# A new table of offsets for the planner that orders a graph network's steps

## The chip, the cores and the metric

The kernel runs on one core of one Trainium2 chip. The core has a matrix engine (TensorE, PE in the profile; its weight loads are PEld), a vector engine (VectorE, DVE), a scalar engine (ScalarE, ACT), GpSimd (POOL) and a queue for transfers (SyncE, SP). Each works through its own list of instructions in order and waits at semaphores for the others. The metric is the device time of one execution in microseconds (us).

## The reference, cut to what matters

The input is 128 graphs of 64 nodes with 128 features, and a weighted adjacency matrix for each. Four layers follow each other, each of them a layernorm, a relu, a graph network and a residual:

- layer 0 makes, for every edge, 64 Gaussians of the edge weight, a softplus of a 64 to 128 matrix product, a second product, and sums neighbours' features times this filter;
- layer 1 works in hyperbolic space: each node's feature is mapped by norms, tanh and artanh; for every edge a silu of a product, a score through a sigmoid, and a weighted sum of logarithmic maps; then a small network, more norms, tanh and silu;
- layer 2 is a product with the normed adjacency matrix, layer 3 messages averaged over neighbours.

```python
h = jnp.maximum(_layernorm(x, axis=-1), 0.0)
x = x + _L0_gnn_ref(h, adj, adj, ...)
...
x = x + _L1_gnn_ref(h, adj, ...)
x = x + _L2_gnn_ref(h, adj, ...)
x = x + _L3_gnn_ref(h, adj, ...)
```

The result is x after the fourth layer, in float32.

## The kernel before, in words

Eight graphs make a group (two graphs on the 128 partitions, four such pairs), and 16 groups are computed. Since few nodes are joined, the nodes of a graph are sorted by degree and each node has a number of slots for its neighbours; the slots come in three blocks, of 512, 512 and 264 columns a pair. Per-edge work runs over these slots. (A second, dense program stands behind a flag, for inputs with too many neighbours; it isn't run here.)

Each group passes seven stages, written as Python generators: `load` (two transfers), `order` (sorting, one-hot tables `oh`), `layer0` (filters per edge), `layer1_nodes` (norms and maps of the nodes), `layer1_edges` (scores per edge), `rest1` (the end of layer 1) and `rest2` (layers 2 and 3, and the store). A stage starts further generators for its parts: `squares`, `duo`, `filter_of` and `neighbours` belong to `layer0`; `coefs_of`, `rows` and `scores_of` to `layer1_edges`; `one_minus_z`, `attention`, `norm_of_h` to `layer1_nodes`; `product_with_h` to `rest1`. A generator's name with a 2 behind it in the table means the third, smaller block of slots.

A generator yields `on(engine, buffers, after=events, table=...)` ahead of each of its steps: on which engine the step runs, which buffers it takes, what must have been issued before, and whether it needs ScalarE's table of logarithm and exponential ("log") or of silu and tanh ("silu"). The class `Weave` plans: it keeps a modelled time for each engine (`free`, advanced by the costs in `about`, from line 785), and `step` (line 940) looks up, for all generators, when their next step could begin. It takes the engine of the earliest one, and among the steps of that engine which could begin within 0.05 us of it the one with the lowest key. The instructions are emitted in that order, and the kernel's scheduler is told to keep it on four engines. At run time nothing chooses: the order is fixed, and waits follow from the data.

The key is set in `Stream.go_on` (line 860):

```python
self.want = next(self.gen, None)
self.key = self.rank + next(self.late, 0.0)
```

`rank` is twice the group's number plus the stage's due time (`load` -6, `order` -4, `layer0` and `layer1_nodes` -3, `layer1_edges` 0, `rest1` 2, `rest2` 4). `late` runs over the entry of the table `LATE` (line 808) for this generator, one offset per step, and gives 0.0 once that is used up. So a positive number lets other steps go first, a negative one draws a step forward. The offsets are the same for every group.

ScalarE's table is switched by the last loop of `sparse_stack`: for each group it goes silu (until `soft_ready`), log (until `soft`, the softplus of the layer 1 nodes), silu (until the scores and `rest1` are through) and log (until the filters of layer 0 and the nodes are through). Steps of the other table wait.

Of the kernel before, what the change touches and what calls it, by code (L numbers as in the profile page):

```python
# [784 lines left out]
def about(engine, op, args, kw):  # L785
# [14 lines left out]
    if engine == ACT:  # L800
# [5 lines left out]


LATE = {
    "attention": (0, 3.75),
    "coefs_of": (2.5, 0, -0.25),  # L810
    "coefs_of2": (2.5,),
    "duo": (4, 4.25),
    "duo2": (0, 3.5, -1.5),
    "filter_of": (1.75, 3.5, 0.25, -0.75, 0, -2.25),
    "filter_of2": (-3.75, 3.5, 0, 4.5, -2.5),
    "layer1_edges": (0, 0, 0, -3),
    "layer1_nodes": (-2.25, 0, 0, 0, 0, 4.5, 0, 4.25, 1.75, 0, 0, 0, 0, 0, 3.5, 0.5, 0, 0, 0, 0, 0,
        0, 0, 0, -1.5, 0, 0, 0, 0, -3.25, 0, 0, 0, 0, 0, 0, -0.5, 0, 0, 0, 0, 0, 0, 3, 0, 0, 3),
    "neighbours": (-0.5, -2),
    "neighbours2": (3.5,),  # L820
    "one_minus_z": (-1.5,),
    "order": (0, 0, -2.25, 0, 0, 0, 4.25, 3.25, 0, -2, 0, 1.75, 0, 2.25, 0, 0, 1.75, 0, 6, -2.25),
    "product_with_h": (0, 2.5),
    "rest1": (0, 0, 0, -3.75, 0, 0, 0, 1, 0, -3.25, 0, 0, 0, 0, -0.5, -2, 0, 0, 0, 0, 0, 0, -1.25),
    "rest2": (0, 0, 0, 0, 0, 0, 0, 0, 0, 0, 0, -3.75, 0, 2, 0, 2.75, 0, 0, 0, 0, 3.5, 0, 0, 0, 0, 0,
        0, 0, 1),
    "rows": (1.25, -2.75),
    "rows2": (1.75, -0.25),
    "scores_of": (0.75, 0, -1.75, -0.5),
    "scores_of2": (0, -1.25),  # L830
    "squares": (2,),
    "squares2": (0, 2.25),
}


# [1422 lines left out]
```

## Time and profile before

| | us |
|---|---|
| median of three runs (2148.49 to 2150.37) | 2149.32 |
| profiled execution | 2152.3 |
| its span, first to last instruction | 2150.5 |
| TensorE matmuls busy in the span | 1826.5 (85%), 11223 instructions |
| VectorE busy | 1832.9 (85%), 4829 instructions |
| ScalarE busy | 1671.5 (78%), 3385 instructions |
| GpSimd busy | 369.7 (17%), 362 instructions |
| ScalarE table loads, in the above | 111.6, 87 loads |

The mean granted TensorE clock is 0.941 of full speed. Almost every instruction is issued by the same helper (line 849, in `Timed`), so rows of the profile are told apart by the names of the tiles. In such a row, `out<-in` names the written and the read tiles, then come partitions x elements, the count, busy time, mean duration of one, and the idle time of the engine ahead of them with what ended it. Names that help here: `e` and `ex` are the Gaussians and the wide activations per edge, `ra` the neighbours' features, `two` the filter product of the third block, `va` weights or coefficients per slot, `th` the tanh of the scores, `oh` the one-hot tables, `rt`, `rs`, `bR`, `n`, `Sx` and `nn` tiles of the layer 1 nodes, `w` and `k_` tiles of `rest1`, `big`, `sm` and `sl` PSUM buffers.

### The profile page before, as it was taken

What the parts mean: (1) busy time and instruction counts of PE and PEld (TensorE: products, weight loads), DVE (VectorE), ACT (ScalarE), POOL (GpSimd) and SP (SyncE); (2) the same over time, 40 slices, a digit from 0 to 9 for tenths busy, and PEclk for the clock granted to TensorE, in tenths of its full rate; (3) what the DMA queues carried; (4) which work ended last, traced back from release to release, by engine and by line L of the source; (5) the groups of instructions that cost most, each with busy time, mean ns of one, the idle gap of its engine ahead of it and who ended that gap; (6) DMA issues with size and microseconds to landing.
All of it is one profiled execution on the core that took longest, in us unless ns stands there. A gap on an engine that the chain in (4) does not pass through costs nothing.

```text
span 2150.5 us, 32066 instructions
## 1 busy us (share of the span) xinstructions
PE 1826.5 (85%) x11223; PEld 873.5 (41%) x11223; DVE 1832.9 (85%) x4829; ACT 1671.5 (78%) x3385; POOL 369.7 (17%) x362
## 2 busy tenths in 40 slices
PE   3767989898999989898999989898999989896773
PEld 2223333443444444443444444443444444433342
DVE  4448889899999989899999989899999999887752
ACT  1968787979879797979879797979879797985541
POOL 1000101122120212122120212222130212202121
PEclk9988999999999999999999999999999999998775
DMA  2000000000000000000000000000000000000000
GB/s 52 5 0 6 1 6 1 1 6 8 6 8 6 8 6 8 1 6 8 6 8 6 8 6 8 1 6 8 6 8 1 8 1 6 1 1 6 5 1 12
DMA packets 29532, 13.95 MB, mean 6 GB/s; under 512 B 10544, under 2 KB 29360, under 8 KB 29360
## 3 DMA queue, kind: packets, MB, share of 16 engines
q1 hardware_dynamic: 29360, 11.80, 2.1%
q8 instruction: 90, 1.47, 0.3%
q14 instruction: 82, 0.67, 0.1%
HBM read 7.61 MB, written 4.19 MB: 5 GB/s over the span
## 4 chain that ended last, share of the span: by engine, by line
PE 41%; ACT 31%; DVE 22%; issue 4%; DMA 1%; POOL 0%; SPq 0%; DVEq 0%; ACTq 0%; POOLq 0%
PE big L849 29%; PE sm L849 9%; ACT ex L849 9%; ACT e L849 5%; DVE va L849 4%; ACT ra L849 4%; PE sl L849 4%; ACT n L849 3%; DVE oh L849 3%; DVE ex L849 2%; DVE ah L849 2%; DVE y L849 2%; ACT va L849 2%; ACT L849 2%; ACT th L849 1%
## 5 line engine op out<-in xcount | busy, mean ns | idle before, releaser
L849 PE MATMUL big<-ex,w2T 128*128 128x512 f32 (+1 forms) x768 | 328.5, 553 | 41.3 <-ACT ex L849 35.0
L849 PE MATMUL big<-e,w1T 64*128 64x512 f32 (+1 forms) x768 | 205.3, 635 | 57.2 <-ACT e L849 52.6
L849 ACT ACTIVATE ex<-big,c_L_gnn_att_b 128x1024 f32<-128x1024 f32 (+1 forms) x192 | 183.3, 968 | 78.0 <-PE big L849 77.4
L849 DVE SCALAR_TENSOR_TENSOR ex<-big,c_L_gnn_b,ra 128x1024 f32<-128x1024 f32 x128 | 163.8, 1280 | 67.8 <-PE big L849 55.6
L849 PEld LDWEIGHTS big<-ex,w2T 128*128 128x128 f32 x768 | 131.2, 190 | 215.7 <-ACT ex L849 93.0
L849 ACT ACTIVATE ex<-big,c_L_gnn_b 128x1024 f32<-128x1024 f32 (+1 forms) x192 | 184.6, 978 | 43.9 <-PE big L849 43.6
L849 PE MATMUL big<-va,U 64*128 64x512 f32 (+1 forms) x768 | 184.7, 558 | 31.8 <-DVE va L849 31.6
L849 PE MATMUL big<-va,a 64*128 64x512 f32 (+1 forms) x768 | 185.5, 579 | 10.3 <-DVE two L849 4.3
L849 PE MATMUL sl<-ex,aw2b 128*64 128x512 f32 (+1 forms) x768 | 180.7, 549 | 8.4 <-ACT th L849 4.5
L849 ACT ACTIVATE ra<-big 128x528 f32<-128x528 f32 (+1 forms) x192 | 167.3, 884 | 17.7 <-PE big L849 17.0
L849 ACT ACTIVATE ex<-ex 128x1024 f32<-128x1024 f32 (+1 forms) x192 | 175.6, 924 | 0.9
L849 DVE TENSOR_REDUCE y<-ex 128x128 f32<-128x1024 f32 x128 | 155.1, 1212 | 0.8
L849 POOL TENSOR_TENSOR k_r<-k_r,exp 128x4 f32<-128x4 f32 x32 | 47.5, 1484 | 580.4 <-DVE k_r L849 568.7
L849 ACT ACTIVATE th<-sl,hab 128x512 f32<-128x512 f32 (+1 forms) x192 | 118.1, 615 | 37.0 <-PE sl L849 35.2
L849 PE MATMUL big<-slot_r,Sx 64*128 64x512 bf16 (+1 forms) x1152 | 137.4, 343 | 0.0
L849 PEld LDWEIGHTS big<-e,w1T 64*128 64x128 f32 x768 | 69.4, 205 | 155.6 <-ACT e L849 65.2
L849 ACT ACTIVATE va<-va,sr 128x512 f32<-128x512 f32 (+1 forms) x192 | 122.5, 649 | 9.0 <-DVE va L849 9.0
L849 PE MATMUL big<-oh,pqs 64*64 64x512 bf16 (+1 forms) x1152 | 122.8, 347 | 0.0
L849 ACT ACT_TABLE_LOAD x87 | 111.6, 1283 | 2.2 <-PEq L2246 0.7
L849 DVE COPY_PREDICATED va<-slot_r,big 128x1024 f32<-128x1024 uint16 (+1 forms) x96 | 106.6, 1111 | 5.3 <-PE big L849 5.1
L849 DVE TENSOR_TENSOR va<-oh,adjT 128x1024 f32<-128x1024 bf16 (+6 forms) x160 | 103.6, 697 | 5.7 <-ACT va L849 4.9
L849 DVE TENSOR_TENSOR oh<-pos,slot_k 128x2048 bf16<-128x2048 bf16 (+6 forms) x128 | 107.7, 849 | 0.2
(470 smaller groups left out, 3799.6 us busy)
## 6 DMA issues: line engine op xcount, KB each, us to landing
x<-in_x_dram SPq DMA_DIRECT2D x16, 256.0 KB, 2.9
out_dram<-v SPq DMA_DIRECT2D x16, 256.0 KB, 2.3
adj<-in_adj_dram SPq DMA_DIRECT2D x16, 128.0 KB, 2.3
e<-in_L_gnn_mlp_w_dram SPq DMA_DIRECT2D x3, 64.0 KB, 1.8
wupd<-in_L_gnn_W_upd_dram SPq DMA_DIRECT2D x1, 128.0 KB, 5.8
e<-in_L_gnn_Wd_dram SPq DMA_DIRECT2D x2, 64.0 KB, 2.9
e<-in_L_gnn_W_dram SPq DMA_DIRECT2D x2, 64.0 KB, 1.8
e<-in_L_gnn_att_w_dram SPq DMA_DIRECT2D x2, 64.0 KB, 1.8
```

Of the source, the lines that this page charges most:

```text
L849: return f(*args, **kw)
```

## The change

Only the table `LATE` is replaced. Generators that had no entry get one (`layer0`, `normed_x`, `product_with_bias`, `weights_of2`), some lose theirs (`attention`, `one_minus_z`, `rows`), and nearly all others have other offsets. Costs, due times, buffers, table switching and all steps stay.

```diff
 LATE = {
-    "attention": (0, 3.75),
-    "coefs_of": (2.5, 0, -0.25),
-    "coefs_of2": (2.5,),
-    "duo": (4, 4.25),
-    "duo2": (0, 3.5, -1.5),
-    "filter_of": (1.75, 3.5, 0.25, -0.75, 0, -2.25),
-    "filter_of2": (-3.75, 3.5, 0, 4.5, -2.5),
-    "layer1_edges": (0, 0, 0, -3),
-    "layer1_nodes": (-2.25, 0, 0, 0, 0, 4.5, 0, 4.25, 1.75, 0, 0, 0, 0, 0, 3.5, 0.5, 0, 0, 0, 0, 0,
-        0, 0, 0, -1.5, 0, 0, 0, 0, -3.25, 0, 0, 0, 0, 0, 0, -0.5, 0, 0, 0, 0, 0, 0, 3, 0, 0, 3),
-    "neighbours": (-0.5, -2),
-    "neighbours2": (3.5,),
-    "one_minus_z": (-1.5,),
-    "order": (0, 0, -2.25, 0, 0, 0, 4.25, 3.25, 0, -2, 0, 1.75, 0, 2.25, 0, 0, 1.75, 0, 6, -2.25),
-    "product_with_h": (0, 2.5),
-    "rest1": (0, 0, 0, -3.75, 0, 0, 0, 1, 0, -3.25, 0, 0, 0, 0, -0.5, -2, 0, 0, 0, 0, 0, 0, -1.25),
-    "rest2": (0, 0, 0, 0, 0, 0, 0, 0, 0, 0, 0, -3.75, 0, 2, 0, 2.75, 0, 0, 0, 0, 3.5, 0, 0, 0, 0, 0,
-        0, 0, 1),
-    "rows": (1.25, -2.75),
-    "rows2": (1.75, -0.25),
-    "scores_of": (0.75, 0, -1.75, -0.5),
-    "scores_of2": (0, -1.25),
-    "squares": (2,),
-    "squares2": (0, 2.25),
+    "coefs_of": (2.25, 1.75),
+    "coefs_of2": (2.25,),
+    "duo": (3.25, 3.75, -3.5),
+    "duo2": (1, 2.5),
+    "filter_of": (2, 5, 0, 0, 0.5, -3),
+    "filter_of2": (-2.75, 2.5, -2.25, 2.75),
+    "layer0": (0, 0, 0, 0.25),
+    "layer1_edges": (0, 0, 0, -3.5),
+    "layer1_nodes": (3.75, 0, 0, 2.25, 3, 3, 0, 2.5, 0, 1.5, 0, 0, 0, 0, 0, 0, 0, 3, 0, 0, 0, 0, -3,
+        0, 0, 0, 0, 0, 0, 0, 0, 0, 0, 0, 0, 2.25, -3.75, 2.25, 0, 0, 0, 0, 0, 0, 0, 0, 3.5),
+    "neighbours": (0, -1.5),
+    "neighbours2": (2.25, 2),
+    "normed_x": (0, 0, 0, 0, -3, 2, -3.5),
+    "order": (0, 0, 0, 0, 2.5, 0, 0, -4.25, 0, 4.25, 0, 0, 4, 0, 2, 0, 0, 2.75, 0, 0, 3.25),
+    "product_with_bias": (0, -0.75),
+    "product_with_h": (0, 2.75),
+    "rest1": (0, 1, 0, -3.5, -1.5, 0, 0, -3.5, -0.75, 0, 0, 0, 0, 0, 0, 0, 0, 0, 3.75),
+    "rest2": (8.75, 0, 0, 0, 0, 0.25, 0, 0, 0, 0, 0, -3.25, 0, 0.5, 0, 2.25, 0, 0, -0.5, 0, 4.25, 0,
+        -4, 0, 1.25, 0, -2.5, 0, 5.25),
+    "rows2": (2, -0.25),
+    "scores_of": (-2.5, 1.75, -3.5),
+    "scores_of2": (0.75, 0, 0, 3),
+    "squares": (3, 7.5),
+    "squares2": (2.75, 0, 0, 3.5),
+    "weights_of2": (0, 0.75),
 }
```

## The prediction

> **What bounds the kernel now.** I read the page's forty slices first, then busy time by stretch, then the waits of the busiest engine, then single instructions.
>
> ```profile
> PE   3767989898999989898999989898999989896773
> DVE  4448889899999989899999989899999999887752
> ACT  1968787979879797979879797979879797985541
> PEclk9988999999999999999999999999999999998775
> ```
>
> Three parts: a lead-in of some four slices, a long even middle, and a drain at the end in which nobody is full. In VectorE's records the first instruction of the edges of group 2 starts at 453.8 us and that of group 13 at 1787.2, so one group takes (1787.2 - 453.8) / 11 = 121.2 us. I cut the span there (columns: PE, PEld, DVE, ACT, POOL busy, granted clock, DMA share, GB/s):
>
> ```profile
> 52.00:139.00 87.00, 60.18 (x246) 22.42 (x247) 41.01 (x59) 79.40 (x86) 0.00 (x0) 0.92 0.01 3
> 139.00:222.00 83.00, 61.01 (x291) 29.03 (x291) 62.41 (x162) 60.58 (x124) 6.54 (x7) 0.81 0.01 4
> 454.00:1787.00 1333.00, 1210.40 (x7700) 575.82 (x7699) 1246.65 (x3284) 1123.21 (x2311) 259.45 (x231) 0.98 0.02 6
> 1908.00:2015.00 107.00, 81.66 (x506) 44.27 (x505) 81.45 (x241) 61.42 (x156) 16.74 (x17) 0.81 0.01 3
> 2015.00:2151.00 136.00, 81.56 (x514) 48.31 (x512) 63.14 (x221) 46.21 (x127) 25.25 (x26) 0.66 0.03 7
> ```
>
> From 52 to 139 us ScalarE is the limit (79.4 of 87 us). In the middle it is VectorE: 1246.65 / 11 = 113.3 us of 121.2, so 7.9 us a group are idle. Of these 4.1 us lie in gaps over 0.15 us; the rest are small gaps between instructions. No order can win more in the middle than these 4.1 us a group. After 1908 no engine is full: a chain of dependent steps sets the time. VectorE's waits in the middle:
>
> ```profile
> DVE ex L849 <- PE big L849: 17.7, 27, 1.1
> DVE ex L849 <- ACT ra L849: 8.5, 11, 0.8
> DVE two L849 <- PE big L849: 6.1, 11, 0.6
> DVE dn L849 <- PE sm L849: 4.7, 10, 0.5
> DVE a L849 <- PE sm L849: 3.0, 11, 0.3
> ```
>
> Eleven of each are eleven periods. In one period (1181 to 1302 us) they stand at 1182.07 (0.44 us), 1212.22 (0.27), 1238.65 (0.47), 1261.96 (0.77), 1267.88 (0.21), 1269.61 (0.55) and 1274.03 (1.05), 3.76 us together.
>
> **What the Trainium skill says.** "PSUM — Partial Sum Buffer", section "Engine vs sequencer instructions": the queues of ScalarE, VectorE and GpSimdE are strict FIFO. So an instruction whose input is late holds all behind it, and the order decides which wait is covered. The trace agrees: at 1186.69 ScalarE idles 4.55 us before a Square on `w`, with scores queued behind it. "ScalarE: Activation LUTs", section "What ACT_TABLE_LOAD costs", gives 1283 ns for a table load and 1380 ns more for a drain. The trace has the same load, but no such drain:
>
> ```profile
> L849 ACT ACT_TABLE_LOAD x87 | 111.6, 1283 | 2.2 <-PEq L2246 0.7
> 81.14 1.28 ACT L849 ACT_TABLE_LOAD   x1
> 82.44 0.70 ACT L849 ACTIVATE ex<-big,c_L_gnn_b 128x528 f32<-128x528 f32 x1
> ```
>
> (the two lower lines are ScalarE's timeline.) The next activation follows 0.02 us after the load ends, so I price a load at 1.283 us.
>
> **The change part by part.** It computes nothing else and adds no instruction of work. On every engine the multiset of steps is the same, the DMA queue's order is the same, and VectorE, ScalarE, PE and POOL agree to the letter in their last 218, 110, 329 and 27 steps of the stream. So no engine gets less work except in one place:
>
> 1. *Lead-in.* There Exp and Ln force a load at each alternation between them, until the first switch to silu. The built program before holds 87 loads, as the trace does; after, 83. All four fewer are in this lead-in (26 against 22), because Exp and Ln now more often run in pairs. 4 x 1.283 = 5.1 us of ScalarE. Its share busy there is 79.4 / 87 = 0.91, so I count 0.91 x 5.1 = 4.7 us gained. Bounds: nothing, if the chain of group 0's nodes (139 to 222, where ScalarE has 22 us free) swallows it; 4 x 2.66 = 10.6 us by the skill's dearer price.
>
> 2. *Middle, twelve periods.* I laid VectorE's new order over one period's timeline.
> Covered now: the 0.44 us at 1182.07, since two `coefs_of` products (1.13 us apart) stand ahead of the `filter_of` product instead of one; and the 0.27 us at 1212.22, since the first softplus step of `layer1_nodes` moves behind `rest1`'s artanh, about 8.3 us of VectorE work later. Together -0.71 us.
> The moved softplus keeps its cover: between its halves stand a reduction and four small products (1.13 + 1.05 us), ScalarE needs 1.29. So does the layernorm after it: ahead of its second half stand 0.64 + 1.13 + 0.78 us, POOL's two steps take 1.45. `x` and `ln_mv` thus come later, but what reads them stands where it stood.
> Added: the clamp of `rt` moves from behind `one_minus_z` to right behind one reduction.
>
> ```profile
> 1277.72 0.29 DVE L849 TENSOR_SCALAR rt<-e 128x256 f32<-128x256 f32 x1
> 1277.93 1.21 DVE L849 TENSOR_REDUCE y<-ex 128x128 f32<-128x1024 f32 x1
> 1279.06 0.28 DVE L849 TENSOR_SCALAR bR<-gr 128x256 f32<-128x256 f32 x1
> ```
>
> ScalarE's Ln and two Exp run from 1278.05 to 1279.37; the clamp would start at 1279.06. That is a new wait of 0.31 us and a hop, +0.35 us; behind it are queued `bR`, `e`, and, through `e`, ScalarE's last Ln.
> Also added: the second step of splitting `Sx` moves from 1295.47 to about 1293.5. Its copy on ScalarE, at 1294.66 now, has 0.7 us less work ahead of it after `xp`, a 0.69 us wait that may go, and about 0.4 us less before `xp`: 1292.9 to 1293.5, and 0.54 us long. A wait of 0 to 0.7 us; I take +0.15, the low side, as the copy's own input now comes earlier as well.
> Nought: `ra`, for which VectorE waits at 1261.96, moves behind one more Ln on ScalarE (+0.53 us), but waits of 0.21, 0.55 and 1.05 us follow within 12 us, and for the first two of them that Ln is earlier. If these don't shrink it costs 0.53.
> The one-hot compares and both first `rows` products of the edges change places; they are needed long after, or leave ScalarE's scores nearer together. Neither shows a VectorE wait.
> Sum -0.71 + 0.35 + 0.15 = -0.21 us a period, x 12 = -2.5 us. Bounds: -3.76 x 12 = -45 us, and about +1.6 x 12 = +19 us.
>
> 3. *Drain.* From 1911.1 ScalarE is on the silu table for the last edges but one; it leaves it for the softplus of group 15 at 1919.44 and idles 1.39 us for VectorE there, after idling 2.71 us for `w`. In the new order two scores and a tanh stand ahead of `w`, and the softplus comes after ten scores and tanhs more. I count both waits as gone: -4.1 us. VectorE now reaches group 15's first node step after 20.9 us more of other work, and its norms (`nn`) after 8.1 us more. In the trace `nn` is ready at 1951.9 us and waits for the log table, which comes only after the last tanh (1962.80), so about 10.9 us are free. POOL's `ln_r` there is moved behind `rest1`'s norms (0.27 + 1.04 us), with the same cover. Bounds -8 and +8 us. From group 15's edges to the end (136 us) hardly a step moves.
>
> Sum: -4.7 - 2.5 - 4.1 = -11.3 us. The profiled execution has a span of 2150.5 us and took 2152.3; that becomes 2139.2 and 2141.0. The median shown is 2149.3, 3.0 under the profiled one: 2149.3 - 11.3 = 2138.0 us. What a measurement can tell from no change is about 0.2%, 4.3 us.
>
> **The rivals.**
> *Slower: the `Sx` split.* For it: VectorE is at its limit, so any wait in the middle is paid twelve times. If the copy stays at 1294.66 while the subtraction comes at 1293.5, VectorE stands until 1295.3: 1.8 us instead of 0.15, +1.65 x 12 = 19.8 us, and -11.3 turns to +8.5: 2157.8 us. It ends slower by over 0.2% from a wait of 0.15 + (11.3 + 4.3) / 12 = 1.45 us on. Against it: the copy has less queued ahead.
> *Nothing measurable.* The four loads are hidden by the node chain (0), `ra`'s 0.53 us isn't absorbed (-2.5 + 6.4 = +3.9), the drain gives 4.1: -0.2 us, 2149. For it: idle ScalarE from 139 on.
> *Much faster.* The later waits shrink as well: half of the 3.76 us, 1.9 x 12 = 22.6, and 8.8 from both ends: -31.4, 2118 us. For it: `ex` and `two` wait for PE work whose order changed in many small ways I can't price. Against: the instructions around those waits on VectorE are unmoved.
>
> **How the numbers follow.** The forecast 0.50, slower 0.20, nothing 0.13, much faster 0.17. The forecast's own range is 2125 to 2146, and little of it falls within 0.2%. Faster 0.65, same 0.14, slower 0.21. The range 2114 to 2159 takes in most of the far cases.
>
> **What would show it.** ScalarE with 83 loads of 1.283 us; the edges of group 0 starting some 5 us before 222.1; the period near 121.0; in it no wait of `ex` at the start of the edges nor of `a`, a new one of `rt` for ScalarE of about 0.35 us, and at most 0.7 us for `Sx`; the last tanh before group 15's log table about 4 us earlier, relative to group 14's edges. A period over 121.6 or a wait for `Sx` over 1.45 us makes the forecast wrong; so does one under 120, or a drain that isn't shorter.

## The result, and the profile after

The new table is slower: a median of 2162.39 us over five runs (2160.24 to 2165.61) against 2149.6 us for the old one beside it (2148.49 to 2152.71), a ratio of 1.0058 with a 95% interval of 1.0043 to 1.0072. The forecast was 2138.0, with a range from 2114 to 2159. The profiled execution has a span of 2163.8 us, 13.3 more than before.

The page of the profile after, busy time and slices:

```profile
PE 1822.3 (84%) x11223; PEld 869.6 (40%) x11223; DVE 1864.7 (86%) x4829; ACT 1665.7 (77%) x3381; POOL 325.4 (15%) x362
...
PE   3768989898989889898998989898998989897773
DVE  4548899999999989999999989999999999988752
ACT  1968697969788797979789796978889796976441
PEclk9979999999999999999999999999999999997775
```

VectorE issues the same 4829 instructions as before and is busy for 1864.7 us instead of 1832.9. A table of offsets can't add work, so instructions have become longer. The same stretches as before, by stages (columns: PE, PEld, DVE, ACT, POOL busy, granted clock, DMA share, GB/s):

```profile
52.00:139.00 87.00, 58.23 (x245) 22.67 (x246) 41.69 (x67) 72.59 (x81) 2.69 (x4) 0.89 0.01 3
449.00:1800.60 1351.60, 1212.55 (x7704) 575.52 (x7700) 1274.43 (x3285) 1125.70 (x2312) 216.11 (x231) 0.97 0.02 6
1921.90:2028.30 106.40, 82.95 (x503) 45.35 (x501) 80.51 (x239) 61.74 (x162) 16.14 (x18) 0.78 0.01 3
2028.30:2163.80 135.50, 78.95 (x516) 46.04 (x512) 64.86 (x225) 45.67 (x124) 24.02 (x26) 0.69 0.03 7
```

Between the first edges instructions of groups 2 and 13 lie 1351.5 us where 1333.4 lay before: 122.9 us a period instead of 121.2. VectorE is busy for 1274.43 / 11 = 115.9 us of it, 2.5 more, and idle for 7.0 instead of 7.9. So the waits did shrink. They are VectorE's own in the middle, in total, times, longest:

```profile
DVE ex L850 <- PE big L850: 10.5, 10, 1.1
DVE ex L850 <- ACT ra L850: 7.9, 11, 0.7
DVE at_p L850 <- ACT at_m L850: 7.1, 9, 0.8
DVE two L850 <- PE big L850: 5.2, 12, 1.4
DVE rt L850 <- ACT rt L850: 2.8, 11, 0.3
```

To see where the time went I use two landmarks of the layer 1 nodes in VectorE's records, which both kernels have once in a group: the subtraction `n<-x,ln_mv`, behind which ScalarE and TensorE have much to do for VectorE, and the scalar-tensor step `e<-gr,h`, some 45 us later. I call the way from the first to the second the *joint part* of the period, and the way on to the next group's `n<-x,ln_mv` the *VectorE part*. Times between landmarks, in us:

| from, to | before | after | difference |
|---|---|---|---|
| start, n of group 2 | 383.2 | 379.0 | -4.2 |
| n of group 2, n of group 13 | 1333.6 | 1350.3 | +16.7 |
| of this, 11 joint parts | 490.6 | 491.3 | +0.7 |
| of this, 11 VectorE parts | 843.0 | 859.0 | +16.0 |
| n of group 13, n of group 14 | 121.5 | 123.9 | +2.4 |
| n of group 14, end | 312.1 | 310.6 | -1.5 |

**Which instructions grew.** Matching VectorE's records of groups 4 to 12 one by one, six differ by more than 0.25 us: a one-hot compare `oh` takes 3.34 us instead of 2.28, the last small product `va` of `weights_of` 1.48 instead of 0.40, a `th` 1.02 instead of 0.17, an `rb` 1.00 instead of 0.16; in return one `th` takes 0.16 instead of 0.67 and a second compare 2.25 instead of 2.62. Beside each of the longer ones runs a step of GpSimd that began 0.07 to 0.29 us before it. The timeline of after, VectorE and GpSimd (start, duration in us):

```profile
1198.38 0.98 DVE L850 TENSOR_SCALAR rb<-beta 128x4 f32<-128x4 f32 x1
1199.49 3.35 DVE L850 TENSOR_TENSOR oh<-pos,slot_k 128x2048 bf16<-128x2048 bf16 x1
1202.92 2.25 DVE L850 TENSOR_TENSOR oh<-pos,slot_k 128x2048 bf16<-128x2048 bf16 x1
1259.30 1.01 DVE L850 TENSOR_SCALAR th<-th 128x4 f32<-128x4 f32 x1
...
1198.30 1.04 POOL L850 TENSOR_TENSOR a<-xp,o_mv 128x512 f32<-128x512 f32 x1
1199.42 1.27 POOL L850 TENSOR_TENSOR xp<-xp,r_L_gnn_bd 128x512 f32<-128x512 f32 x1
1259.01 1.27 POOL L850 TENSOR_TENSOR x<-x,r_L_gnn_b 128x512 f32<-128x512 f32 x1 [6.49 <-ACT v L850]
```

`rb` handles 4 numbers a partition and ends with GpSimd's `a` (1199.36 and 1199.34); `th` ends with GpSimd's `x` (1260.31 and 1260.28). The compare is 1.10 us longer than its twin right behind it, beside a GpSimd step that still had 1.20 us to go. `va`, at 1243.55, stands the same way beside GpSimd's `n` (1243.40 to 1244.76). The Trainium skill names a mechanism that fits, in "SBUF — State Buffer", section "Who interferes with whom": VectorE and GpSimd share a pair of ports as an exclusive lock, and in certain kinds of instruction the second one to issue blocks until the first is finished. The durations agree with it. The same two compares and the same `rb` in before:

```profile
1183.70 2.28 DVE L849 TENSOR_TENSOR oh<-pos,slot_k 128x2048 bf16<-128x2048 bf16 x1
1192.17 2.59 DVE L849 TENSOR_TENSOR oh<-pos,slot_k 128x2048 bf16<-128x2048 bf16 x1
1204.40 0.16 DVE L849 TENSOR_SCALAR rb<-beta 128x4 f32<-128x4 f32 x1
```

**What the TensorE clock did.** The trace's records of the clock show it at full or at half speed, changing on a grid of 3.41 us whose phase stays the same through a run. In the middle, from n of group 2 to n of group 13, every half-clock stretch of the two kernels but one lies in the joint part. The busy time by stretch, first two joint parts of before, then two of after:

```profile
1110.56:1155.52 44.96, 38.38 (x239) 18.95 (x235) 39.52 (x118) 41.80 (x98) 8.32 (x7) 0.92 0.00 1
1232.14:1276.28 44.14, 37.24 (x239) 18.49 (x235) 39.41 (x118) 41.56 (x98) 8.33 (x7) 0.96 0.00 1
```

```profile
1237.60:1282.41 44.81, 37.48 (x235) 18.36 (x229) 40.42 (x118) 41.36 (x98) 8.38 (x7) 0.92 0.00 1
1607.54:1651.35 43.81, 36.44 (x235) 17.91 (x229) 40.22 (x117) 41.23 (x98) 8.41 (x7) 0.96 0.00 1
```

The granted clock, the third number from the end, is 0.96 with one step of 3.41 us at half clock and 0.92 with two; the second step costs the joint part 0.8 to 1.0 us. In before, one and two alternate (its period of 121.2 us is 35.5 grid steps). In after two come in eight of eleven periods, in a row: 122.75 us is nearly 36 steps (122.88), so a period meets the grid at almost the place where the last one did.

So two causes stood to be tried, blocking by GpSimd and the clock, beside the order itself.

### The profile page after: what moved, and what is told of

It is laid out like the page before. It is cut to its first block, busy times and chain, and to the rows that moved or that the text cites. A ratio compares the mean times of both kernels' runs of the same rounds, so it can differ in the third digit from the quotient of the medians.

```text
span 2163.8 us, 32015 instructions
## 1 busy us (share of the span) xinstructions
PE 1822.3 (84%) x11223; PEld 869.6 (40%) x11223; DVE 1864.7 (86%) x4829; ACT 1665.7 (77%) x3381; POOL 325.4 (15%) x362
## 4 chain that ended last, share of the span: by engine, by line
DVE 51%; PE 24%; ACT 15%; issue 8%; DMA 1%; POOL 0%; SPq 0%; DVEq 0%; ACTq 0%; POOLq 0%
PE big L850 16%; DVE va L850 9%; PE sm L850 7%; DVE th L850 5%; DVE ex L850 4%; DVE y L850 4%; ACT e L850 3%; DVE att L850 3%; ACT n L850 3%; ACT ex L850 3%; DVE ah L850 2%; DVE v L850 2%; DVE n L850 1%; DVE rt L850 1%; ACT L850 1%
## 5 line engine op out<-in xcount | busy, mean ns | idle before, releaser
L850 ACT ACTIVATE ra<-big 128x1024 f32<-128x1024 f32 (+1 forms) x192 | 166.2, 886 | 21.8 <-PE big L850 21.8
L850 PE MATMUL big<-oh,pqs 64*64 64x512 bf16 (+1 forms) x1152 | 122.7, 347 | 0.0
L850 DVE TENSOR_TENSOR va<-oh,adjT 128x1024 f32<-128x1024 bf16 (+6 forms) x160 | 117.1, 782 | 1.7 <-ACT va L850 1.0
L850 DVE TENSOR_TENSOR oh<-pos,slot_k 128x2048 bf16<-128x2048 bf16 (+6 forms) x128 | 116.8, 919 | 0.2
L850 PEld LDWEIGHTS big<-va,a 64*128 64x128 f32 x768 | 73.7, 207 | 97.9 <-issue 52.8
L850 DVE SCALAR_TENSOR_TENSOR th<-th,oh 128x1024 f32<-128x1024 f32 (+1 forms) x80 | 100.2, 1252 | 10.2 <-ACT th L850 10.2
```

The costliest lines, as they stand in the source:

```text
L850: return f(*args, **kw)
```

## The experiments

A kernel named after_... has the new table, before_... the old one. Every time is compared with before in the same batch (medians 2149.37, 2149.42 and 2150.55).

**GpSimd steps left out.** Three steps stay in the plan, so that the order doesn't move, but aren't issued: in `order` the addition of `bd2s` to `xp`, in `layer1_nodes` the product with `hb`, in `rest2` the addition of `b2g` to `x2`. The result lacks these.

```diff
         def issue(*args, **kw):
+            planned_only = kw.pop("planned_only", False)
...
             kw.pop("share", None)
+            if planned_only:
+                return None
             return f(*args, **kw)
...
-            G.tensor_tensor(xp, xp, bm(bd2s, NP), ALU.add)
+            G.tensor_tensor(xp, xp, bm(bd2s, NP), ALU.add, planned_only=True)
...
-            G.tensor_tensor(tmp, mx, bm(hb, NP), ALU.mult)
+            G.tensor_tensor(tmp, mx, bm(hb, NP), ALU.mult, planned_only=True)
...
-        G.tensor_tensor(x2, x2, bm(b2g, NP), ALU.add)
+        G.tensor_tensor(x2, x2, bm(b2g, NP), ALU.add, planned_only=True)
```

> The new table, with three of GpSimd's wide additions and products left out (the layer 0 bias on xp, the layer 2 bias on x2, the product of the nodes with the bias hb; the planner still counts them, so every other engine keeps its order; the output lacks these terms). Theory of the shared port: VectorE's one-hot compare, its last small weights product and its artanh-like tensor_scalar on th lose 1.06 + 1.08 + 0.85 = 2.99 us a group that they spend blocked by GpSimd; VectorE's busy time a group falls from 115.9 to about 112.9 us, the period from 122.9 to 120.0 to 120.6, the time to 2127 to 2137 us. Theory that the new order itself is worse (later inputs, more waits): the period stays at 122.3 or more and the time at 2155 or more.

Measured: 2159.71 us (2152.36 to 2161.12), ratio 1.0053 [1.0036, 1.0069]: nearly as slow as with them.

> The old table with the same three GpSimd instructions left out (same terms missing from the output). Theory of the shared port: only 0.35 us of the one-hot compare and 0.51 us of a tensor_scalar on th are given back, 0.86 us a group: period 121.2 to about 120.4, time about 2139 us (2135 to 2146), so it is 5 to 12 us slower than the new table without them: with GpSimd out of the way the new order wins by its lead-in (4.7 us) and its smaller waits. Theory that the new order is worse: it stays at least 8 us faster than the new table without them.

Measured: 2146.07 us, ratio 0.9985 [0.9978, 0.9992], 3.3 us less. A miss: it was to be 5 to 12 us slower than after_pool3 and is 13.6 us faster. Of the 0.86 us a period that was to be given back, only the 0.51 us of `th` was; the compare still takes 2.6 us. And the period stayed where it was, at 121.2 us: what VectorE saved there it now waits.

In after_pool3 the lengthened `oh`, `va` and `th` are gone (VectorE is busy for 113.0 us a period), and the VectorE part falls from 77.95 to 76.87 us. But the joint part now takes two values:

```profile
1105.14:1151.02 45.88, 39.09 (x235) 19.14 (x229) 38.79 (x118) 41.42 (x98) 5.75 (x5) 0.89 0.00 1
1227.87:1271.25 43.38, 36.25 (x235) 17.85 (x230) 38.47 (x117) 41.09 (x98) 5.74 (x5) 0.96 0.00 1
```

Eight of eleven periods have three half-clock steps and take 122.7 to 122.9 us; three have one and take 120.3 to 120.4, less than any of before. The sequence within the run tells more: two short periods, five long, one short, then long again. A period of 120.4 is 35.3 steps, so the pattern walks over the grid until it meets a place with three half-clock steps; these stretch the period to 36.0 steps, and the next one meets the same place. With the blocking as the only cause the time should have fallen by the 2.9 us a period that VectorE's instructions shrank. That theory falls in this form, and the times are those that were named for a worse order. The new theory: the clock takes the gain back.

**One table load for both functions.** In the lead-in, where Exp and Ln alternate, the explicit load of the log table was put behind the first ScalarE copy of the plan instead of ahead of it. The tables loaded fall to 65 in both kernels, from 87 and 83.

```diff
-            return f(*args, **kw)
+            out = f(*args, **kw)
+            if self.name == ACT and self.weave.now is not None and self.weave.first is not None:
+                self.engine.preload_act_table_set(self.weave.first)
+                self.weave.first = None
+            return out
...
+        name = {"log": "natural_log_exp_and_others", "silu": "silu_and_others"}[table]
+        if self.table is None:
+            self.first = name
+        else:
+            scalar.preload_act_table_set(name)
         self.table = table
-        scalar.preload_act_table_set({"log": "natural_log_exp_and_others",
-                                      "silu": "silu_and_others"}[table])
```

> The old table, all work kept; only ScalarE's first load of the log table stands behind the first copy of a sorted group instead of at the very start, so that Exp and Ln of the lead-in share one table: 67 loads instead of 87. If a load in the lead-in is worth what step 1 of the prediction says (0.91 of 1.283 us), 20 fewer give 23.3 us: about 2126 us, and the edges of group 0 start at about 199 us. If the lead-in is set by the node chain or by VectorE, less than 10 us: 2140 or more.

Measured: 2124.24 us, ratio 0.9886 [0.9869, 0.9902]. The edges of group 0 start at 192.7 us, where 199 was named.

> The new table with the same single change to the first table load: 16 or so fewer loads than its 83. By step 1's price 0.91 x 1.283 x 18 = 21 us less than the new table: about 2141 us. Since both tables then have the same loads in the lead-in, what is left between them and the old table with this change is the middle and the drain: the new one should be about 16 to 18 us slower (the middle alone), not 12.5.

Measured: 2145.23 us, ratio 0.9977 [0.997, 0.9984].

22 loads fewer bring 25.1 us in the old order, 1.14 us a load, near step 1's price of 0.91 x 1.283 = 1.17. In the new order 18 fewer bring 17.2 us. Between the two profiled executions the span falls by 20.4 us: n of group 2 comes 23.5 us earlier (355.5 for 379.0), and the middle took 1353.3 us instead of 1350.3, with 22 half-clock steps for 20. (The medians differ by less: the profiled execution of after took 2165.6 us, over its median of 2162.4.) What the two tables differ by isn't the lead-in: without its alternating loads the distance is larger, 21 us, where 16 to 18 were expected.

**TensorE kept busy over its pause.** Some 7 us into the joint part TensorE stands for 3.2 us in every period, while ScalarE loads the log table, and the half-clock stretch begins in this pause or just behind it. TensorE's timeline there, one line of before, then after (in brackets the idle time ahead):

```profile
1242.84 3.62 PE L849 MATMUL big<-e,w1T 64*128 64x512 f32 x8 [3.17 <-ACT e L849]
```

```profile
1243.94 0.67 PE L850 MATMUL sl<-ex,aw2b 128*64 128x264 f32 x4
1247.76 3.78 PE L850 MATMUL big<-e,w1T 64*128 64x512 f32 x8 [3.15 <-ACT e L850]
1251.33 2.98 PE L850 MATMUL big<-va,a 64*128 64x512 f32 x8
```

Twelve spare matmuls (the fill, from here on) were put there, into the PSUM tile that the next product overwrites, unknown to the planner, so that the order is the same:

```diff
             pre = big()
+            if w.fresh and g >= 2:
+                for _ in range(12):
+                    nc.tensor.matmul(pre[:, 0, :], lhsT=bones_b, rhs=slot_r[:, 0:512], start=True, stop=True)
+            w.fresh = False
```

(`w.fresh` is set when the log table is loaded. The records show eleven of the twelve.)

> The old table, with twelve spare matmuls (512 columns, bf16, into a PSUM tile that the next matmul overwrites) put on TensorE's queue ahead of the first filter product after each load of the log table, groups 2 and on; nothing else changes, the planner's order is the old one. Theory A (the clock: each period TensorE stands 3.2 us while ScalarE loads the log table, and then runs at half clock for one or two steps of 3.41 us, and each step costs the period about 1.0 us): the stretches in the middle go, the stage from VectorE's step n to its step e falls from 44.06 and 45.05 in turn to about 43.1, the period from 121.2 to about 119.7, 11 periods x 1.5 = 16.5 us: about 2133. Theory B (the stretches of half clock cost nothing that the queues do not hide): 2149 or, with the matmuls in the way, a few us more.

Measured: 2131.36 us (2129.65 to 2134.68), ratio 0.9916 [0.9899, 0.9932]. Theory A holds: the period falls from 121.24 to 120.06 us, where 119.7 was named. The pause in before_warm, the same eight products now 1.99 us long:

```profile
1107.73 0.67 PE L850 MATMUL sl<-ex,aw2b 128*64 128x264 f32 x4
1108.56 2.54 PE L1556 MATMUL big<-slot_r,bones_b 128*128 128x512 bf16 x11 [0.16 <-issue]
1111.58 1.99 PE L850 MATMUL big<-e,w1T 64*128 64x512 f32 x8 [0.48 <-ACT e L850]
```

> The new table with the same twelve spare matmuls. Theory A: the new table's period, 122.75, is so near to 36 steps of 3.41 us (122.88) that nearly every period has two half-clock steps; without them the stage from n to e falls from 44.8 to about 42.9 and the period to 120.8, 11 x 1.95 = 21 us: about 2141, and the distance to the old table under the same edit shrinks from 13 to about 8 us, what the GpSimd blocking leaves (78.0 against 76.6 us a period, less a lead-in shorter by 4.7). Theory B (the new order's chain through ScalarE and TensorE is longer in itself): no gain, 2160 to 2165.

Measured: 2167.06 us (2165.42 to 2167.62), ratio 1.0082 [1.0065, 1.0099]. A miss: the new order gained nothing and took 4.7 us more than without the fill. The filled pause no longer halves the clock, but 14 half-clock steps remain in the eleven periods, nearly all 22 to 26 us into the joint part, where TensorE waits twice:

```profile
1138.66 1.16 PE L851 MATMUL big<-qd,hh 64*128 64x128 f32 x16 [1.69 <-ACT e L851]
1141.40 3.78 PE L851 MATMUL big<-ex,w2T 128*128 128x512 f32 x4 [1.58 <-DVE ex L851]
```

The `ex` of the second wait runs on VectorE from 1140.07 to 1141.35, a little behind a blocked `th`: 1.25 us long from 1138.13 on, where the same instruction takes 0.16 in before, and beside it GpSimd's `x` from 1138.10 to 1139.37.

> The new table, the three GpSimd additions and products left out as in after_pool3 (so the result lacks two biases and one product), and the twelve spare matmuls. Theory A: both causes gone: 76.9 us from e to n and about 42.4 from n to e, a period of 119.3, so 11 x 3.2 = 35 us below after_pool3: about 2124, and faster than the old table under the same clock edit (2133) by some 8 us. Theory B: as after_pool3, 2159.

Measured: 2123.78 us (2121.37 to 2125.42), ratio 0.988 [0.9863, 0.9896]. With the three steps and nearly all half-clock steps gone the new order is 25.6 us faster than the old kernel, and faster than the old order under the fill.

> The old table, the log table's first load placed behind the first ScalarE copy (as in before_onetable, 2124.2) and the twelve spare matmuls. Theory A: the two gains add: about 2124 - 16.5 = 2108, below both kernels. Theory B: 2124.

Measured: 2106.70 us (2103.67 to 2108.07), ratio 0.9806 [0.979, 0.9822]. The two gains add up (25.1 and 18.1 us apart, 42.7 together), and this is the best complete kernel found: the old table, one table load fewer at each alternation, and a TensorE that isn't let stand.

**Which of the three steps it is.** The same fill, with some or all of the three left out.

> The new table and the twelve spare matmuls, with only the GpSimd addition of b2g to x2 left out (one bias is missing from the result). Theory A: this one holds up VectorE's small th steps between n and e, and these hold up ex and so TensorE, which pauses 1.6 us and drops to half clock a second time; without it the stage from n to e falls from 44.2-45.5 to about 42.3-42.9, the stage from e to n keeps the two other lengthened steps, 77.95; the period is about 120.4 and the time 2167 - 11 x 2.6 = about 2138. Rival: the held-up th is hidden like the other waits of that stage and the two others carry the loss: 2160 or more.

Measured: 2158.56 us (2155.5 to 2159.6), ratio 1.0039 [1.0028, 1.0051]. A miss. The joint part is shorter by what was blocked, but a half-clock step now comes in ten of eleven periods at another place, just behind `e<-gr,h`:

```profile
1037.98 0.27 PE L854 MATMUL sm<-last_d,bones_b 128*128 128x256 bf16 x1 [1.25 <-ACT n L854]
1038.09 0.27 PE L854 MATMUL sm<-pos,bones 128*128 128x256 bf16 x1
1038.88 1.92 PE L854 MATMUL sm<-v,r 64*64 64x128 f32 x16 [0.52 <-DVE o L854]
```

The products at 1038.88, 1.09 us long in before_warm, take 1.92. At full clock this order's period would be 121.25 us; the half-clock step adds 1.6 and makes it 122.88, which is 36 steps, and from 547.5 us on the step recurs every 122.9 us to the end of the middle. The same wait of TensorE stands in the other kernels with the new table; it halves the clock only where the grid falls badly.

> The new table and the twelve spare matmuls, with the GpSimd addition of bd2 and the product with b_lin left out and b2g kept (a bias and a product are missing from the result). Theory A: the stage from e to n falls from 77.95 to 76.87, the stage from n to e stays at 44.2 to 45.5 with its second half-clock stretch: a period of about 121.9, so 2155 (2145 to 2160). Rival: these two carry the loss: 2130 or less.

Measured: 2133.01 us (2131.94 to 2136.01), ratio 0.9926 [0.9906, 0.9946]. A miss too, and nearer to the rival: these two steps carry the larger part, and a period of 120.0 us (35.2 steps) doesn't lock.

> The old table with the three GpSimd steps left out and the twelve spare matmuls. In the old order these steps lengthen VectorE by only 0.5 us a period, between n and e, where it is hidden: about 2131 - 3 = 2128, as before_pool3 stood 3 us under before. Then the new order, at 2123.8 under both edits, is some 4 us the better of the two, which is what its shorter lead-in brings, and the middle is level or better by less than 0.5 us a period.

Measured: 2129.99 us (2129.32 to 2130.23), ratio 0.9908 [0.9889, 0.9926]. As expected within 2 us, and level with before_warm. With both causes gone in both, the new order is some 5 to 6 us the faster (2123.8 against 2130.0, in batches whose runs of before differ by 1.1).

All of it in one table, from the traces. Times in us, means of groups 2 to 12; "at full clock" is the sum of the median joint part and the median VectorE part among those without a half-clock step:

| kernel | median | joint part | VectorE part | period | half-clock steps in 11 periods | period at full clock |
|---|---|---|---|---|---|---|
| before | 2149.4 | 44.60 | 76.64 | 121.24 | 17 | none seen |
| before_pool3 | 2146.1 | 44.61 | 76.62 | 121.23 | 17 | none seen |
| before_warm | 2131.4 | 43.41 | 76.66 | 120.06 | 2 | 120.01 |
| before_pool3_warm | 2130.0 | 43.39 | 76.63 | 120.02 | 2 | 119.99 |
| after | 2162.4 | 44.66 | 78.09 | 122.76 | 20 | none seen |
| after_pool3 | 2159.7 | 45.27 | 76.87 | 122.13 | 27 | none seen |
| after_warm | 2167.1 | 44.89 | 78.10 | 122.99 | 14 | 122.14 |
| after_b2g_warm | 2158.6 | 43.38 | 79.42 | 122.80 | 10 | 121.25 |
| after_two_warm | 2133.0 | 43.22 | 77.32 | 120.55 | 7 | 119.98 |
| after_pool3_warm | 2123.8 | 42.34 | 77.18 | 119.52 | 2 | 119.17 |

(The profiled execution of after_pool3 took 2152.4 us; the three others, at 2158 to 2161, show a lower mean clock, 0.930 to 0.932 instead of 0.936. The grid lies differently against the start of each trace, so one order may have executions with more and with fewer half-clock steps; no kernel was traced twice to show it.)

The last column adds up. Leaving out b2g takes 0.89 us off 122.14, leaving out the two others takes 2.16 off, all three 2.97, and 0.89 + 2.16 = 3.05. VectorE's busy time a period falls by 1.09, 2.20 and 3.27 us (from 115.98 in after_warm), so in the new order blocked time is paid in the period almost one to one. A rival would be that a left-out step shortens the chain of data and not VectorE's instructions; then VectorE's idle time would have to shrink, and it is 7.0 us a period with the three steps and 6.8 without.

In the old order the same kind of blocking was free. Its `th` at 1254.27 is also lengthened, to 0.67 us. But the chain of work that ended last runs through ScalarE there; in the new order it runs through the blocked `th` (the views of the chain, before, then after):

```profile
1253.96 0.59 ACT e L849
1254.55 0.41 ACT va L849
1254.95 0.53 ACT e L849
```

```profile
1259.08 0.19 DVE th L850
1259.30 1.01 DVE th L850
1260.41 0.17 DVE th L850
```

That fits before_pool3: VectorE's busy time a period fell by 0.54 us, its idle time rose by 0.53, and the period moved by 0.01.

## Why the prediction was wrong

**Step 1, lead-in (-4.7): right.** There are 83 loads of 1.283 us, ScalarE's busy time from 52 to 139 us fell by 6.8, and n of group 2 comes 4.2 us earlier, the edges of group 2 4.7 (449.1 for 453.8). It shows later than named: the edges of group 0 start at 222.0 us for 222.1, not some 5 us earlier, and those of group 1 4.1 us earlier.

**Step 2, middle (-2.5): wrong, and most of the miss lies here.** From n of group 2 to n of group 14 it came to +19.1 us, 21.6 of the 24.7 us by which the sum was off. The waits behaved much as laid out. The waits of `ex` at the start of the edges and of `a` are gone; the clamp of `rt` waits for 0.25 us (predicted 0.35); the split of `Sx` waits for nothing, so the rival "slower" fell with its mechanism, though its number, 2157.8, was the nearest. One wait was overlooked: `at_p` for ScalarE's copies, 0.8 us, which now have a copy of `ra` ahead of them. VectorE's waits over 0.15 us went from 4.1 to 3.3 us a period. The term that failed stands in none of the sums: that a VectorE instruction keeps its duration wherever it is put. "So no engine gets less work except in one place" was read as "no instruction gets longer", and moving GpSimd's steps past VectorE's was priced at nothing. At full clock blocking costs the new order 2.97 us a period by the three steps alone, against 0.02 in the old one (120.01 of before_warm less 119.99 of before_pool3_warm; in before_warm these three steps lengthen no VectorE instruction by more than 0.15 us). Without these steps the new order is better by 119.99 - 119.17 = 0.82 us a period, more than the 0.21 predicted, although `rb` is still blocked for 0.84 us there by a fourth GpSimd step, which wasn't tried. The net at full clock is 122.14 - 120.01 = +2.13 us a period.

Measured is 122.76 - 121.24 = +1.52. The rest is the clock: half-clock steps add 1.23 us to the old order's period and 0.62 to the new one's. These shares are good to some tenths only, as the fill also shifts which `th` meets GpSimd's addition (1.02 us long in after, another one 1.25 in after_warm). So the clock didn't make the new table slower than the old; on balance it hid a part of the loss. What it did do was to take back the gain where the blocking alone was removed: at full clock -2.97, measured -0.63 in the profiled executions, with 27 half-clock steps for 20.

The forecast's bound rests on the same term. "No order can win more in the middle than these 4.1 us a group" counts VectorE's idle time as all that there is to gain, and takes its busy time as fixed. No order was found that won more, but the busy time isn't fixed: under the fill the old order's period fell by 1.2 us, of which VectorE's busy time made 0.63 (113.24 to 112.61, mostly the `th` that was no longer blocked) and its idle time 0.54.

**Step 3, drain (-4.1): -1.5 from n of group 14 to the end.** ScalarE's wait for `a` on VectorE (1.4 us) is gone. Its two waits for `w` on TensorE changed from 2.7 and 6.6 us to 1.2 and 8.1, the same sum. New are 4.2 us for VectorE's `s`, where it waited 0.2, and 1.9 for `w` on VectorE. TensorE ran at half clock for 47.8 us from 1977 on instead of 17.1 + 23.9 from 1967 on, but from n of group 14 to the end its half-clock time is no longer than before (137.5 us for 141.5), so the clock alone doesn't explain what is missing. So the two waits named were shortened and the time turned up in others; on a chain of dependent steps a wait that goes isn't a gain until what stands behind it is also earlier. Which step held the drain back wasn't tried.

The sum as it came: -4.2 + 16.7 + 2.4 - 1.5 = +13.4 us, where -11.3 was forecast. The chance of 0.21 for slower had the sign by luck: its mechanism took no part in it.

## What to carry to other kernels

When an order is changed, a duration from the old profile holds only for the neighbours the instruction had there: for every GpSimd step that moves, look at which VectorE instruction will run beside it, and price the pair, at worst, at one behind the other; it counts where that instruction stands on the chain that ends last. Where TensorE's clock is granted by its recent use, look for its pauses before counting anybody else's waits, and fill a pause that recurs with matmuls nobody needs; in the old order that was worth 18 us, more than the 11.3 that had been hoped for from the whole new table, and in the new one nothing until the blocking was gone too. And if taking away a proven cost changes nothing, don't drop the cost: look for what answers to the new timing.

## What the runs showed of the hardware

*The clock's rule.* In thirteen traces, between 350 and 1850 us, I set TensorE's busy share in each grid step of 3.41 us against the clock of the next step. Of 5517 steps at full clock, all 111 that were busy for less than 0.49 were followed by half clock; of the 5380 at 0.50 or more, 5373 were followed by full clock and 7, between 0.50 and 0.61, by half; of the 26 in between 8 were followed by half clock. Of 180 steps at half clock 56 were followed by another, none of them busy for more than 0.88, and 124 by full clock, none busy for less than 0.86. (The ends of matmuls are modelled in the records, so the shares are good to some hundredths.) The Trainium skill describes the gate in "TensorE: Matmul & The Clock Gate", section "What's actually happening": half rate by default, a free-running window of 3413 ns, lowered after an idle window. The traces agree on both clocks and on the window; but no idle window is needed here, one that is busy for just under half (0.48) is enough.

*Locking to the grid.* A loop whose period comes near a whole number of these steps keeps its half-clock steps: 36 steps are 122.88 us, and after_b2g_warm and after_pool3 fall into it from 121.25 and 120.4 us, because the slow steps themselves make up the difference. In before, at 35.5 steps, one and two slow steps take turns instead.

*Blocking can be added to the period in full, though the engine has idle time.* In the new order at full clock 1.09, 2.20 and 3.27 us less of VectorE's busy time moved the period by 0.89, 2.16 and 2.97 us, although VectorE had some 7 us of idle time in each. In the old order 0.54 us less moved it by 0.01, where ScalarE had the chain.
